# Regrouping the output products of a cross-attention kernel: A12·B21 in the queries' PSUM bank, S2·T2 on top of P1, and the fourth batch's x one slot sooner

## The chip, the cores and the metric

The kernel runs on one core of a Trainium2 chip. The number of interest is the device time of one execution in microseconds. The core has five engines that run their own instruction queues in order: TensorE (PE, with its weight loads shown as PEld), VectorE (DVE), ScalarE (ACT), GpSimd (POOL) and SyncE (SP), which here only issues DMAs. They wait for each other by semaphores. All data is float32.

## The reference

For eight batches of 256 rows and 1024 features the kernel computes layer norm, a query projection, attention of 32 heads over a context that serves as keys and as values, an output projection and the residual sum:

```python
x = (hidden_states - mu) * jax.lax.rsqrt(var + LN_EPS) * ln_gamma + ln_beta
Q = _split_heads(x @ Wq.T)
K = _split_heads(memory_keys)
V = _split_heads(memory_values)
scores = jnp.einsum('bhsd,bhtd->bhst', Q, K) * scale
scores = jnp.where(mask, scores, -jnp.inf)
probs = jax.nn.softmax(scores, axis=-1)
attn = jnp.einsum('bhst,bhtd->bhsd', probs, V)
out = attn.transpose(0, 2, 1, 3).reshape(B, S, HIDDEN) @ Wout.T
return residual + out
```

## The kernel before

**Slots.** The work is cut into 64 slots, eight for each batch; a slot handles one group of four heads (128 features). The loop `for n in range(N)` writes the instructions of slot n, and since every engine takes its instructions in order, the order of this text is the order of the work. The scheduler is off (`manual_schedule`), so nothing is reordered. In slot n PE first computes the scores of group n+1 (`scores`, L479), then the values of group n-2 (`values`, L622), and around them parts of other products; meanwhile DVE, ACT and POOL do the softmax of group n+1 (`softmax_parts`).

**Softmax.** `exps` is a DVE pass with the mask (L515) and an ACT exponential (L519) for each half of four heads; `normalize` is a DVE reciprocal (L526) and two POOL multiplications (L528); `blocks` transposes with DVE (L534) into pT, and `aside` copies a part with ACT into pc (L540). The `tail` then lets SP swap partition quarters by DMA: two pT<-pT (L600), then two pT<-pc (L604). Between the two pairs SP issues the loads listed in `between`, which fills the wait for the first pair. `values` of a group can start only when its pT is complete. `copy_at` moves a group's values from PSUM to SBUF (ACT, L635).

**Queries.** For batches 0 to 2 `make_q` (L340) multiplies plain blocks of x with Wq; ACT copies the result out with `copy_q` (L347 to L353). From batch 3 on the query projection is a seven-product form of the 2x2 block product (`query_product`, L440): one product a slot in seven of eight slots, emptied by `copy_product` (L450, L456, L461). All go through one PSUM bank, pool `ps_q`; the second halves made during batch 0 and 1 use the output bank, pool `ps_o`. The x of a batch is loaded some eleven slots ahead (`load_x`, L130), its statistics are DVE work (`ln_stats`, L226), its rearrangement is DMA work (`move_x`, L327).

**Output projection.** For each batch, in the eight slots after its own attention began to finish, `product_steps` (L694) runs seven products of four matmuls each: P1 = A11·B11, A12·B21, S2·T2, S3·T3, A22·T4, S1·T1, S4·B22. Here A are quarters of the attention output, B quarters of Wout, and S and T are sums of them (`sum_at` on POOL L675, `sum_wo` on POOL L183). The four quarters of the result are: C11 = P1 + A12·B21; the other three are P1 + S2·T2 plus further products. `STEPS` gives for each slot i of the batch how many steps stand before the values, after them, and at the slot's end. In every batch but the last two, A12·B21 is added in the bank that holds P1. `keep_p1` (ACT, L702) copies P1 to SBUF first; S2·T2 then starts a new bank, and POOL adds the kept P1 to three quarters of the residual (`add_p1`, L727). `store`, `take` (DVE, L732 to L736) add a bank to the residual tile r, and `store` also sends it.

**Order around the change.** In slot i=1 of a batch the order on PE is scores, four A11, values, three A12; in slot i=2 scores, values, the last A12, the query product, two S2. `copies` stands for the emptying of query banks: early in the softmax in the first eight groups, at its end later. The loads of Wout (`load_wo`), of x, of k, v and of the residual (`load_res`) are put into `between` of chosen slots, in this order.

Of the kernel before, what the change touches and what calls it, by code (L numbers as in the profile page):

```python
# [59 lines left out]
def xattn_kernel(  # L60
# [11 lines left out]
    nc = tc.nc  # L72
# [4 lines left out]
    NQ = NC  # L77
# [160 lines left out]
        else:  # L238
            later.append(pow_)

    def ln_norm(b, s, engine):
        if engine is nc.scalar:
            shift = sm.tile([P, 1], F32, tag="shift", name=f"shift_{b}_{s}", bufs=2)
            nc.gpsimd.tensor_scalar(
                shift, mvs[b][:, s, 0:1], rstds[b][:, s : s + 1], -1.0, ALU.mult, ALU.mult
            )
            engine.activation(
                xs[b][:, s, :], xs[b][:, s, :], AF.Identity,
                bias=shift, scale=rstds[b][:, s : s + 1],
            )  # L250
            return
        engine.tensor_scalar(
            xs[b][:, s, :], xs[b][:, s, :], mvs[b][:, s, 0:1], rstds[b][:, s : s + 1],
            ALU.subtract, ALU.mult,
        )

# [234 lines left out]
    def softmax_parts(n, copies=(), ahead=(), between=(), hooks={}, fill=()):  # L491
# [50 lines left out]
        if n == 0:  # L542
            for j in range(NH - 1):
                exps(j, (0,))
            yield
            exps(NH - 1, (0,))
            fill_in()
            yield
            for j in range(NH):
                exps(j, (1,))  # L550
            normalize(0)
            fill_in()
        else:
            exps(0)
            while tails:
                tails.pop()()
            late = "p1" in hooks
            if not late:
                for done in list(pvs):
                    copy_at(done)  # L560
            exps(1)
            for hook in hooks.get("soon", ()):
                hook()
            exps(2)
            normalize(0)
            for hook in hooks.get("p1", ()):
                hook()
            exps(3)
            if late:
                for done in list(pvs):  # L570
                    copy_at(done)
        if n <= NQ:
            for copy in copies:
                copy()
        for hook in hooks.get(0, ()):
            hook()
        normalize(1)
# [10 lines left out]
        blocks(2)  # L588
        while fill:
            fill_in()  # L590
        if n > NQ:
            for copy in copies:
                copy()

        def tail():
            blocks(3)
# [48 lines left out]


    PRODUCTS = (
        ("A11", B11, True), ("A12", B21, False), ("S2", T2, True), ("S3", T3, False),
        ("A22", T4, False), ("S1", T1, True), ("S4", B22, False),
    )  # L650

    STEPS = ((0, 0, 0), (4, 0, 3), (0, 1, 2), (0, 2, 2), (0, 2, 1), (0, 1, 2), (0, 0, 3), (0, 1, 2),
             (0, 2, 0))
    ENDS = ((0, 0, 2), (0, 0, 5), (0, 0, 5)) + ((0, 0, 4),) * 4 + ((0, 0, 0),)
    ENDS_TO = {2: (0, 0), 3: (0, 1), 4: (1, 1), 5: (1, 0), 6: (1, 1), 7: (0, 1)}
# [18 lines left out]
            operand(b, name)[:, c], operand(b, one)[:, c], operand(b, two)[:, c], op  # L676
        )

    s2s, p1s = {}, {}

    def product_steps(b, steps):
        for step in steps:
            p, c = divmod(step, NK)
            name, which, begins = PRODUCTS[p]
            po = pos.get(b)
            if b == B - 2 and name in ("A12", "S2"):

                begins = name == "A12"
                if begins and c == 0:
                    po_q[0] = ps_q.tile([P, 512], F32, tag="pq", name=f"po_{b}_{name}")  # L690
                po = po_q[0] if begins else po
            elif begins and c == 0:
                po = pos[b] = ps_o.tile([P, 512], F32, tag="po", name=f"po_{b}_{name}")
            nc.tensor.matmul(  # L694
                po, operand(b, name)[:, c], wo[:, which, c],
                start=begins and c == 0, stop=c == NK - 1,
                skip_group_check=not begins,
            )
# [3 lines left out]
        nc.scalar.copy(p1s[b], pos[b])  # L702


    po_q, ends_kept = [None], {}

    def copy_po(b, i):
        if "tile" not in ends_kept:
# [3 lines left out]
        nc.scalar.copy(ends_kept[i], pos[b])  # L712

    def take_po_q(b):
        nc.vector.tensor_tensor(p1s[b], po_q[0], p1s[b], ALU.add)
        ends_kept[2] = p1s[b]

    def add_kept(b, i, s, h):
# [10 lines left out]
    def take(b, s, h):  # L729

        r = rs[b, s, h]
        nc.vector.tensor_tensor(r, pos[b], r, ALU.add)  # L732

    def store(b, s, h, po=None):
        r = rs.pop((b, s, h))
# [54 lines left out]
    for b in range(1, B):  # L790
        first = NQ * (b - 1) + 2
        if b == 1:
            when = dict(moves=())
        elif b == 2:
            when = dict(
                loads=(0, 1), stats=(2, 3), norms=(3, 3), trans=(4, 5),
                moves=tuple(5 + (i + 2) // 6 for i in range(16)),
            )
        else:
            when = dict(  # L800
                loads=(first - 12, first - 11) if b == SPLIT else (first - 13, first - 12),
                stats=(first - 10, first - 9) if b == SPLIT else (first - 11, first - 9),
                norms=(first - 8, first - 7), trans=(first - 7, first - 6),
                moves=tuple(first - 6 + (i + 2) // 6 for i in range(16)),
            )
# [12 lines left out]
        if b % 2 == 0:  # L818
            masks[NQ * b - 7].append(b)
# [30 lines left out]

    ln_stats(0, 0)
    ln_stats(0, 1, (0,))
    ln_norm(0, 0, nc.vector)
    ln_stats(0, 1, (1, 2))
    transpose_x0(0)
    early, late = (0, 1, 5, 2, 6, 3), (7, 4)
    for c in early + late:
        copy_x0(0, c, nc.vector if c > 4 else nc.scalar)
    nc.gpsimd.tensor_copy(xnT0[:, :, S], bet)
    ln_norm(0, 1, nc.vector)  # L860
    first_q(0, early + late)
    mask_bias(0)
    transpose_x0(1)
# [20 lines left out]
    for b in range(B - 1):  # L884
        done, ends = 0, b == B - 2
        for i, counts in enumerate(ENDS if ends else STEPS):
            n = NQ * (b + 1) + i
            for place, k in enumerate(counts):
                steps.setdefault((n, place), []).append((b, range(done, done + k)))
                done += k  # L890
        for i, *what in (
            ((2, keep_p1), (3, take_po_q), *((i, copy_po, i) for i in range(3, 8))) if ends else
            ((1, keep_p1), (2, store, 0, 0), (3, take, 0, 1), (4, take, 1, 1), (6, store, 1, 0),
             (7, store, 1, 1), (8, store, 0, 1))
        ):
            evacuations[NQ * (b + 1) + i].append((what[0], b, *what[1:]))
# [6 lines left out]
    for n in range(N):  # L903
# [8 lines left out]
        if n + 3 in firsts or n + 2 in firsts:  # L912
            between, ahead = between + ahead, []
        if b >= 0:
            if b == B - 2 and i - 1 in (5, 6):
                between.append(partial(send, b, *ENDS_TO[i - 1]))
            if i < 4 and b + i > 0:
                between.append(partial(load_res, b, *((0, 0), (0, 1), (1, 1), (1, 0))[i]))
        between += [partial(load_x, *args) for args in loads[n]]
        between += [partial(load_mask, one) for one in masks[n]]  # L920
        for which, pair in {
            0: ((B12, 0),), 1: ((B22, 0),), 2: ((B11, 0), (B12, 1)), 3: ((B22, 1),),
            4: ((B11, 1), (B21, 0)), 5: ((B21, 1),),
        }.get(n, ()):
            between.append(partial(load_wo, which, pair))
        if n == NQ - 2:
            between.append(partial(load_res, 0, 0, 0))
        if n == N - 4:
            again = xp.tile([P, NS, D], F32, tag="x", name="x_again")
# [22 lines left out]
        if n in products:  # L952
            query_product(*products[n])
            copies.append(partial(copy_product, *products[n]))
        for one in now:
            one()
        fill = []
        if n < 2:
            transpose_x1(2 * n)
# [5 lines left out]
        if n + 1 < N:  # L965
            softmax(n + 1, copies, ahead, between, hooks, fill)
        else:
            copy_at(n - 2)
            for load in between:
                load()  # L970
        if b >= 0 and i == 1:
# [30 lines left out]
        if b == B - 2:  # L1002
            if i > 2:
                add_kept(b, i, *ENDS_TO[i])
        elif b >= 0 and i in (3, 4, 5):
            add_p1(b, *{3: (0, 1), 4: (1, 1), 5: (1, 0)}[i])
        for one in later:
            one()
        if n in halves and n % 2:
# [32 lines left out]
    )  # L1042
    end_steps(to_c11, "A12", B21, (0,), (0,))
    end_steps(to_c21, "A22", T4, (0,), (0,))
    end_steps(to_c22, "S1", T1, (0,), (0,))
    end_steps(to_c11, "A12", B21, (1,))
    end_steps(to_c21, "A22", T4, (1,))
    values(N - 2)
# [8 lines left out]
    copy_at(N - 1)  # L1057
    end_sum(slice(3, 4), nc.vector)
    first_cols, last_cols = slice(0, 384), slice(384, 512)
    end_steps(to_c22, "S1", T1, (1,))  # L1060
    end_steps(s2t2, "S2", T2, (2,))
    for r in (r01, r10, r11):
        end_add(r, s2t2)
# [61 lines left out]
```

## Time and profile before

| | |
|---|---|
| median of 3 runs | 577.23 us (575.44 to 579.26) |
| the profiled execution's own time | 577.06 us |
| its span in the profile | 575.3 us, mean granted clock 0.997 |
| PE busy | 567.5 us, 99% of the span |
| DVE busy | 459.1 us, 80% |
| ACT busy | 411.6 us, 72% |
| POOL busy | 403.8 us, 70% |
| DMA | 117.98 MB, mean 205 GB/s |

Busy time is a sum over the span; matmuls are pipelined, so a busy PE is not PE at its peak. The span is the profiled execution from its first to its last instruction; its own time is 1.8 us longer. A line such as "PE po_A L694 <- ACT qa L349: 2.7, 1, 2.7" in the view of waits says who waited for whom, how long in all, how often, and the longest. In the chain of work each line gives start, length and the instruction that had to end before the next could go on. In the timeline a line gives start, length, engine, source line, operation, tiles, shapes and, in brackets, the idle time of the engine before it and what ended it. A 128x512 matmul is recorded as two records, a group of values as 64.

### The profile page before, as it was taken

The numbers are of one execution on the slowest core, as the hardware profiler recorded it, in microseconds if no ns is written. First come the engines' busy times: TensorE is split into PE (matmuls) and PEld (weight loads), VectorE is DVE, ScalarE is ACT, GpSimd is POOL, SyncE is SP. The second block draws the span as 40 slices with busy tenths as digits, with TensorE's granted clock in tenths as the row PEclk, the third lists the DMA queues.
The fourth block names the chain that finished last, engine by engine and source line by source line (L and its number), as shares of the span: only waits on it lengthen the run. The fifth ranks groups of instructions, "written<-read, shape, count | busy, mean of one in ns | idle before, by whom it ended". The sixth has DMA issues, their size and how long they took to land.

```text
span 575.3 us, 20001 instructions
## 1 busy us (share of the span) xinstructions
PE 567.5 (99%) x7162; PEld 393.2 (68%) x7162; DVE 459.1 (80%) x1696; ACT 411.6 (72%) x1424; POOL 403.8 (70%) x675
## 2 busy tenths in 40 slices
PE   8999998999999999999999999999999999999997
PEld 8778884667667777677676677667766767755444
DVE  5897986888877879889888888888877868879824
ACT  3697886677667867698667967778766876769820
POOL 1788896899896896766567675666657657448780
PEclk9999998999999999999999999999999999999999
DMA  8667877666778677877677776897568865536751
GB/s 303 233 191 234 236 223 200 203 194 187 191 235 270 202 199 194 252 227 222 182 230 230 214 204 195 241 272 203 144 182 267 241 196 138 140 107 180 205 163 74
DMA packets 47475, 117.98 MB, mean 205 GB/s; under 512 B 9104, under 2 KB 9872, under 8 KB 47376
## 3 DMA queue, kind: packets, MB, share of 16 engines
q1 hardware_dynamic: 47088, 116.69, 68.8%
q8 instruction: 57, 0.93, 0.7%
q14 instruction: 42, 0.34, 0.2%
q10 hardware_dynamic: 288, 0.01, 0.0%
HBM read 65.28 MB, written 11.53 MB: 134 GB/s over the span
## 4 chain that ended last, share of the span: by engine, by line
PE 84%; DMA 4%; POOL 4%; DVE 3%; ACT 2%; issue 1%; SPq 1%; DVEq 0%; ACTq 0%
PE po_S L694 20%; PE pq_A L440 16%; PE po_A L694 11%; PE pv L622 11%; PE sc L479 10%; PE pq L340 7%; PE pq_S L440 6%; PE po_end L761 2%; POOL e L528 2%; DMA wq<-in_wq_dram 2%; DMA x<-in_x_dram 1%; DVE e L515 1%; ACT e L519 1%; DVE pT L534 1%; PE po_last L761 1%
## 5 line engine op out<-in xcount | busy, mean ns | idle before, releaser
L528 POOL TENSOR_SCALAR e<-e,rden 128x256 f32<-128x256 f32 x512 | 235.7, 478 | 129.5 <-DVE rden L526 127.5
L519 ACT ACTIVATE e<-e,mn 128x256 f32<-128x256 f32 x512 | 254.0, 500 | 49.4 <-DVE mn L515 48.3
L534 DVE STREAM_TRANSPOSE pT<-e 128x512 f32<-128x512 f32 x256 | 180.7, 707 | 54.0 <-POOL e L528 34.8
L515 DVE CUSTOM_DVE_ANT_0 e<-sc,mb 128x256 f32<-128x256 f32 x512 | 186.0, 416 | 24.2 <-PE sc L479 23.6
L540 ACT COPY pc<-pT 128x512 f32<-128x512 f32 x128 | 79.0, 617 | 72.1 <-DVE pT L534 42.4
L519 ACT ACTIVATION_READ_ACCUMULATOR e<-e,mn 128x1 f32 x512 | 97.8, 191 | 0.0
L340 PE MATMUL pq<-xnT,wq 128*128 128x256 f32 (+1 forms) x368 | 84.1, 382 | 0.0
L340 PEld LDWEIGHTS pq<-xnT,wq 128*128 128x128 f32 x368 | 68.7, 190 | 14.3 <-issue 4.0
L479 PEld LDWEIGHTS sc<-k,qa 32*128 32x128 f32 x1024 | 46.1, 184 | 42.4 <-issue 22.0
L622 PE MATMUL pv<-pT,v 64*32 64x128 f32 x4096 | 74.5, 274 | 0.2
L622 PEld LDWEIGHTS pv<-pT,v 64*32 64x32 f32 x4096 | 57.0, 105 | 25.6 <-issue 11.6
L694 PE MATMUL po_S<-wo,at 128*128 128x512 f32 x152 | 74.3, 606 | 0.0
L479 PE MATMUL sc<-k,qa 32*128 32x256 f32 x1024 | 73.6, 400 | 0.1
L694 PE MATMUL po_A<-wo,at 128*128 128x512 f32 x128 | 62.4, 622 | 2.7 <-ACT qa L349 2.7
L694 PE MATMUL po_S<-wo,s 128*128 128x512 f32 x104 | 50.1, 605 | 0.0
L526 DVE RECIPROCAL rden<-den 128x2 f32<-128x2 f32 x256 | 37.7, 147 | 6.6 <-ACT e L519 5.3
L515 DVE DVE_READ_ACCUMULATOR2_ANT mn<- 128x1 f32 x512 | 42.7, 83 | 0.0
L694 PEld LDWEIGHTS po_A<-wo,at 128*128 128x128 f32 x128 | 23.2, 195 | 28.3 <-issue 23.2
L440 PEld LDWEIGHTS pq_A<-xnT,wq 128*128 128x128 f32 x320 | 37.3, 192 | 4.8 <-issue 4.1
L694 PEld LDWEIGHTS po_S<-wo,at 128*128 128x128 f32 x152 | 25.8, 190 | 19.8 <-issue 19.3
L440 PE MATMUL pq_A<-xnT,wq 128*128 128x128 f32 x320 | 37.3, 275 | 0.0
L635 ACT COPY at<-pv 128x128 f32<-128x128 f32 x128 | 26.1, 253 | 9.6 <-PE pv L622 9.6
(95 smaller groups left out, 605.9 us busy)
## 6 DMA issues: line engine op xcount, KB each, us to landing
v<-in_kv_dram SPq DMA_DIRECT2D x32, 512.0 KB, 4.6
pT<-pT SPq DMA_DIRECT2D x128, 128.0 KB, 2.9
pT<-pc SPq DMA_DIRECT2D x128, 128.0 KB, 4.1
ring<-kept_T SPq DMA_DIRECT2D x18, 512.0 KB, 5.3
k<-in_kv_dram SPq DMA_DIRECT2D x32, 256.0 KB, 4.2
x<-in_x_dram SPq DMA_DIRECT2D x14, 512.0 KB, 5.6
r<-in_x_dram SPq DMA_DIRECT2D x28, 256.0 KB, 4.7
out_dram<-r SPq DMA_DIRECT2D x28, 256.0 KB, 3.4
```

What stands on the lines that cost most here:

```text
L340: nc.tensor.matmul(pqs[n], wq[:, o, c, :], xnTs[b](c), start=(c == 0), stop=(c == NC - 1),)
L440: nc.tensor.matmul(pqs[b][:, o, :], w[:, c], x_[:, c], start=begins and o + c == 0, stop=c == NK - 1, skip_group_check=True,)
L479: nc.tensor.matmul(scs[n][j][:, s, :], qa[r, n % NQ, ts(s, P)], ks[n - n % 2][r, n % 2, :], start=True, stop=True,)
L515: nc.vector.tensor_tensor_reduce(out=e[:, s, :], in0=pss[j][:, s, :], in1=mbs[n // NQ], scale=1.0, scalar=NO_SCORE, op0=ALU.add, op1=ALU.m ...
L519: nc.scalar.activation(e[:, s, :], e[:, s, :], AF.Exp, bias=mn[:, s : s + 1], scale=-1.0, accum_out=den[:, s : s + 1],)
L526: nc.vector.reciprocal(rden, dens[j])
L528: nc.gpsimd.tensor_scalar(es[j][:, s, :], es[j][:, s, :], rden[:, s : s + 1], 1.0, ALU.mult, ALU.mult,)
L534: nc.vector.transpose(pT[:, :, :, j, :, :].rearrange("p a i s k -> p (a i) s k"), es[j].rearrange("p s (b t) -> p b s t", t=K),)
L540: nc.scalar.copy(pc[:, :, ts(j, 2)], pT[:, 1, :, ts(j, 2)])
L622: nc.tensor.matmul(pvs[n][r][j * HD : (j + 1) * HD], vs[n - n % 2][ts(r, 2 * K), i, ds(n % 2 * P + j * HD, HD)], pT[ts(r, 2 * K), :, i, j, ...
L635: nc.scalar.copy(ats[b, k][:, c, :, ts(r, 2), :], pv.rearrange("p a s k -> p s a k"))
L694: nc.tensor.matmul(po, operand(b, name)[:, c], wo[:, which, c], start=begins and c == 0, stop=c == NK - 1, skip_group_check=not begins,)
```

## The change

Seven things are different:

- A12·B21 gets its own bank in every batch: the queries' bank, `ps_q`. S2·T2 is added on top of P1 in the output bank. P1 therefore is added by POOL only to quarter (0, 0), in slot i=2, and DVE's new `take_q` adds the A12·B21 bank to the same quarter.
- That quarter is sent from the `between` list of slot i=3 instead of at once.
- `STEPS`: slot i=1 runs all of A11 and three of A12 after the values, slot i=2 the last A12 and two S2 before the query product. In batch 1 the query product of slot 17 stands between A11 and A12.
- In the softmax the copy of values goes back ahead of the second exponential in all slots, the copy of P1 goes behind the last one, and the query copies of slots with that copy, and the first one of slot 8, go ahead of the rest.
- Batch 3's x is loaded in slots 5 and 6 instead of 6 and 7; four pieces of Wout and the first residual tile are loaded one slot later.
- At the start x of batch 0 is normalised in halves.
- At the end the last slot's copy of a result goes behind the copy of values, and the first S1·T1 step of the last batch goes behind the last values.

```diff
@@ softmax_parts @@
-            late = "p1" in hooks
-            if not late:
-                for done in list(pvs):
-                    copy_at(done)
+            for done in list(pvs):
+                copy_at(done)
             exps(1)
             for hook in hooks.get("soon", ()):
                 hook()
             exps(2)
             normalize(0)
-            for hook in hooks.get("p1", ()):
-                hook()
             exps(3)
-            if late:
-                for done in list(pvs):
-                    copy_at(done)
-        if n <= NQ:
-            for copy in copies:
-                copy()
+        for hook in hooks.get("p1", ()):
+            hook()
+        copies = list(copies)
+        for copy in copies[: NQ if n <= NQ or "p1" in hooks else 1 if n == NQ + 1 else 0]:
+            copies.remove(copy)
+            copy()
...
-        if n > NQ:
-            for copy in copies:
-                copy()
+        for copy in copies:
+            copy()
@@ products and steps @@
-        ("A11", B11, True), ("A12", B21, False), ("S2", T2, True), ("S3", T3, False),
+        ("A11", B11, True), ("A12", B21, True), ("S2", T2, False), ("S3", T3, False),
...
-    STEPS = ((0, 0, 0), (4, 0, 3), (0, 1, 2), (0, 2, 2), (0, 2, 1), (0, 1, 2), (0, 0, 3), (0, 1, 2),
+    STEPS = ((0, 0, 0), (0, 7, 0), (0, 3, 0), (0, 2, 2), (0, 2, 1), (0, 1, 2), (0, 0, 3), (0, 1, 2),
@@ product_steps @@
-            if b == B - 2 and name in ("A12", "S2"):
-
-                begins = name == "A12"
-                if begins and c == 0:
-                    po_q[0] = ps_q.tile([P, 512], F32, tag="pq", name=f"po_{b}_{name}")
-                po = po_q[0] if begins else po
+            if name == "A12":
+
+                if c == 0:
+                    po_q[b] = ps_q.tile([P, 512], F32, tag="pq", name=f"po_{b}_{name}")
+                po = po_q[b]
...
+    def take_q(b, s, h):
+        r = rs[b, s, h]
+        nc.vector.tensor_tensor(r, po_q[b], r, ALU.add)
@@ loads @@
-                loads=(first - 12, first - 11) if b == SPLIT else (first - 13, first - 12),
+                loads=(first - 13, first - 12),
...
-            0: ((B12, 0),), 1: ((B22, 0),), 2: ((B11, 0), (B12, 1)), 3: ((B22, 1),),
-            4: ((B11, 1), (B21, 0)), 5: ((B21, 1),),
+            0: ((B12, 0),), 1: ((B22, 0),), 2: ((B11, 0),), 3: ((B12, 1),),
+            4: ((B22, 1), (B11, 1)), 5: ((B21, 0),), 6: ((B21, 1),),
         }.get(n, ()):
             between.append(partial(load_wo, which, pair))
-        if n == NQ - 2:
+        if n == NQ - 1:
             between.append(partial(load_res, 0, 0, 0))
@@ start @@
-    ln_norm(0, 0, nc.vector)
+    for h in range(2):
+        ln_norm(0, 0, nc.vector, ts(h, 512))
...
@@ evacuations and the loop @@
+            if (b, i) == (1, 1):
+                counts = (0, 4, 3)
...
-            ((1, keep_p1), (2, store, 0, 0), (3, take, 0, 1), (4, take, 1, 1), (6, store, 1, 0),
+            ((1, keep_p1), (2, take_q, 0, 0), (3, take, 0, 1), (4, take, 1, 1), (6, store, 1, 0),
...
+            if b < B - 2 and i == 3:
+                between.append(partial(send, b, 0, 0))
...
-        for one in now:
-            one()
+        if n + 1 < N:
+            for one in now:
+                one()
...
             copy_at(n - 2)
+            for one in now:
+                one()
...
-        elif b >= 0 and i in (3, 4, 5):
-            add_p1(b, *{3: (0, 1), 4: (1, 1), 5: (1, 0)}[i])
+        elif b >= 0 and i == 2:
+            add_p1(b, 0, 0)
@@ end @@
-    end_steps(to_c22, "S1", T1, (0,), (0,))
...
-    end_steps(to_c22, "S1", T1, (1,))
+    end_steps(to_c22, "S1", T1, range(2), (0,))
```

More of the change, by code (lines that the diff above doesn't have):

```diff
@@ L239, in ln_stats, with ln_norm @@
             later.append(pow_)
-    def ln_norm(b, s, engine):
+    def ln_norm(b, s, engine, cols=slice(0, D)):
         if engine is nc.scalar:
@@ L252, in ln_norm @@
         engine.tensor_scalar(
-            xs[b][:, s, :], xs[b][:, s, :], mvs[b][:, s, 0:1], rstds[b][:, s : s + 1],
+            xs[b][:, s, cols], xs[b][:, s, cols], mvs[b][:, s, 0:1], rstds[b][:, s : s + 1],
             ALU.subtract, ALU.mult,
@@ L677, in sum_at @@
         )
-    s2s, p1s = {}, {}
+    s2s, p1s, po_q = {}, {}, {}
     def product_steps(b, steps):
@@ L702, in keep_p1 @@
         nc.scalar.copy(p1s[b], pos[b])
-    po_q, ends_kept = [None], {}
+    ends_kept = {}
     def copy_po(b, i):
@@ L714, in take_po_q @@
     def take_po_q(b):
-        nc.vector.tensor_tensor(p1s[b], po_q[0], p1s[b], ALU.add)
+        nc.vector.tensor_tensor(p1s[b], po_q[b], p1s[b], ALU.add)
         ends_kept[2] = p1s[b]
@@ L859, in xattn_kernel @@
     nc.gpsimd.tensor_copy(xnT0[:, :, S], bet)
-    ln_norm(0, 1, nc.vector)
+    for h in range(2):
+        ln_norm(0, 1, nc.vector, ts(h, 512))
     first_q(0, early + late)
```

## The prediction

> **What bounds the kernel now.** I read the engine totals, then the waits of TensorE, then the chain of work where the one long wait lies. The totals:
>
> ```profile
> span 575.3 us, 20001 instructions
> PE 567.5 (99%) x7162; PEld 393.2 (68%) x7162; DVE 459.1 (80%) x1696; ACT 411.6 (72%) x1424; POOL 403.8 (70%) x675
> ```
>
> Busy PE alone proves nothing, so who PE waited for in the whole run:
>
> ```profile
> PE po_A L694 <- ACT qa L349: 2.7, 1, 2.7
> PE busy L120 <- POOL ring masks.py:199: 1.3, 1, 1.3
> PE po_end L761 <- POOL ring L753: 0.4, 1, 0.4
> ```
>
> Three waits, 4.4 us together. Everywhere else PE has its next matmul ready: the inner batches repeat every 68.1 us (po_A starts at 233.30 and 301.42 us in the chain), with no idle PE. So a change to another engine is worth nothing until it moves one of these waits, and a new wait on PE is paid in full. The long one, in the chain of work:
>
> ```profile
> 90.48 0.59 DVE st L226
> 91.07 0.61 DVE pT L534
> 91.68 0.01 DVE rden L526
> 91.69 0.02 issue
> 91.72 0.62 ACT pc L540
> 92.33 0.39 ACT qa L349
> 92.72 0.04 issue
> 92.76 5.26 PE po_A L694 x8
> ```
>
> The first A11 product of slot 9 needs a bank that ACT empties at 92.7, behind DVE, which stood 2.7 us for x:
>
> ```profile
> DVE st L226 <- DMA x<-in_x_dram: 2.7, 1, 2.7
> ```
>
> The stretches around it (busy us of each engine, granted clock, DMA share, GB/s) show a second price:
>
> ```profile
> 88.80:92.70 3.90, 1.23 (x17) 0.72 (x16) 3.47 (x9) 0.98 (x3) 1.81 (x4) 0.98 1.02 288
> 92.70:96.20 3.50, 3.44 (x5) 1.57 (x6) 3.41 (x17) 3.04 (x12) 3.50 (x5) 0.54 0.52 136
> ```
>
> The clock is 0.54 after the gap. The eight records take 5.26 us, the same eight 3.63 in later batches: 1.63 more. This place costs 2.73 + 1.63 = 4.36 us.
>
> **The change part by part.** Matmuls stay the same in number; their places change. Prices on PE, from the chain at 230 to 260 us: scores 1.08, values 1.09, one 128x512 matmul 0.86, a query product 3.57, and 0.19 whenever full matmuls follow scores or values (po_A 3.63 for four after scores, 3.44 without).
>
> *One run of output steps.* Slot i=1 was scores, A11, values, A12; it becomes scores, values, A11, A12, with one change to full matmuls instead of two: -0.19 in each of six batches. For the four inner batches, 2 to 5, that is -0.76; batches 0 and 1 are summed below.
>
> *Slot 9 (batch 0).* Three edits remove the old wait: x is loaded a slot sooner, so DVE need not stand; ACT copies the first query bank before its other work; A11 stands behind the values. What is late next? The values of head group 7, now first, and the transfers that complete pT_7. The queue of SP:
>
> ```profile
> 81.63 1.16 SPq L600 DMA_DIRECT2D pT<-pT  x2
> 82.84 0.58 SPq L136 DMA_DIRECT2D k<-in_kv_dram  x1
> 83.46 0.45 SPq L130 DMA_DIRECT2D x<-in_x_dram  x1
> 83.95 0.43 SPq L150 DMA_DIRECT2D r<-in_x_dram  x1
> 84.48 1.15 SPq L604 DMA_DIRECT2D pT<-pc  x2
> ```
>
> The two pT<-pc at the end complete pT_7. By the trace's semaphore counts fifteen of the second one's sixteen parts have landed at 90.3 and the last at 92.4. Today nobody cares: the values start at 97.95. After the change PE is ready for them at 90.0. And the moved loads stand in this queue: in this group x stays (its other half), the residual (256 KB) goes a slot later and a 512 KB piece of Wout takes its place. That is 256 KB more ahead of pT<-pc; at the 288 GB/s of the row above, 0.9 us. So the copies land at 93.3, or at 91.2 if no part is a straggler.
>
> From there PE has 1.09 + (0.19 + 4x0.86) + 3x0.86 = 7.3 us of slot 9, where before slot 10 began at 101.81. With 93.3 slot 10 begins at 100.6 if the clock stays full and at 102.3 if it is halved for the same 3.4 us, in which 1.7 are lost. [...] I go by the row: 102.3, a loss of 0.5. Bounds: 97.3 (copies in time) is a gain of 4.5; a landing 1 us later still with the gate is a loss of 1.5.
>
> *Slot 8.* The same shift puts 512 KB of x ahead of the pT<-pc issued at 75.71, which landed by 80.8. At the same 288 GB/s that is 1.8 us: 82.6, against values that start at 82.41. I take 0.0, since part of the queue then drained (transfers ran above 350 GB/s near 76); bounds 0 to 1.0.
>
> *Other moved DMAs.* Four of the eight Wout pieces go one slot later. The last, of B21, now leaves SP near 84 and would land near 91 (6.5 us, the median of such loads); its first reader, A12's third matmul, comes near 98 at the soonest. The residual of batch 0 lands in slot 8 and is first read in slot 10. The output of r00 is no longer sent in slot i=2 but in the group of slot i=3, behind pT<-pT and v and ahead of the next residual: 0.53 us of SP issue, taken from one slot and put in the next. Cover: SP stands up to 4.4 us for pT<-pT in such groups. Each at 0.
>
> *Slot 17 (batch 1)* holds a query product in the same queries' bank that A12 now wants. PE: 160.59 + 1.08 + 1.09 + 3.63 + 3.45 = 169.84. ACT's copy took 170.14 to 170.62, 0.2 after the product ended; now A12 waits for it: 169.84 + 0.2 + 0.48 + 0.07 = 170.6, a wait of 0.75. Queued behind it are A12 and all the next scores. Less the 0.19: +0.5. Bounds 0.3 to 1.0.
>
> *The new wait in slot i=2.* The query product there needs the bank that A12 leaves only when DVE has added it to r00 (take_q). Before, the old store read another bank and nothing queued behind it. In batch 2: slot 25 starts at 232.16 and lasts 8.38, so slot 26 starts at 240.54, A12 ends at 243.76, S2's two matmuls at 245.48, and then pq_S may wait. DVE in slots 25 and 26 now:
>
> ```profile
> 238.16 0.71 DVE L534 STREAM_TRANSPOSE pT<-e 128x512 f32<-128x512 f32 x1 [1.65 <-PE pv L622]
> ...
> 243.11 0.41 DVE L515 CUSTOM_DVE_ANT_0 e<-sc,mb 128x256 f32<-128x256 f32 x1
> ...
> 244.48 0.69 DVE L736 TENSOR_TENSOR r<-po_A,r 128x512 f32<-128x512 f32 x1
> ```
>
> The 1.65 us wait for pv goes, as values come first. Then ACT's exps (234.19 + 8x0.495 + 0.4 for the copy of values put ahead = 238.55) and POOL set the last transpose at 240.4; statistics take 1.6 (to 242.0), four score passes 1.4 (to 243.4), then A12's end at 243.8, then 0.7: take_q ends at 244.5, 1.0 us before PE asks. With today's DVE times it would end at 245.17, still 0.3 early. So 0; bounds 0 to 0.7 a batch.
>
> *Covered work.* S2 is read 3.6 us sooner: POOL finished it at 242.09, PE asks at 243.76. Keep_p1 now follows all exps, until 239.2 against 243.76. POOL loses two of three adds of P1 a batch (2x1.28 us), all beside PE: 0. The one it keeps, behind S4, falls in 2.41 us of idle time. Without the cover it would be 1.28 a batch.
>
> *Start and end.* x is normalised in halves; the transposes begin at 7.72, when PE's 32 warming matmuls end (7.9), while the whole normalisation ended at 6.92: 0, at most -0.25. At the end a product that waited for POOL is put behind the last values: -0.43, bounds -0.5 to 0.
>
> *Sum:* +0.5 - 0.76 + 0.5 - 0.43 = -0.2. The profiled run took 577.06 (span 575.3 and 1.8 around it), so 576.9; the median of the runs is 577.23, 0.17 above it: **577.0**. Within 1% (5.8 us) is about what a measurement of this kernel can tell from no change.
>
> **The rivals.** *The transfers are in time (0.20).* If pT_7 has landed by 90.0, slot 9 gains 4.5: 577.23 - 4.5 - 0.76 + 0.5 - 0.43 = 572.0, and 571.4 with the halves at the start and less wait in slot 17. For it: fifteen of sixteen parts were there at 90.3, and the copies were issued while x still moved. Against it: the DMA share of 1.02, and more bytes ahead.
>
> *take_q is late (0.34), the slower case.* Place: the query product of slot i=2, six batches. It decides once take_q ends after PE's request, 1.0 us later than worked out, and then every us is paid six times, with all PE work queued behind. If DVE or r00's landing is 2.5 us late (DVE stood 2.9 us once for a transfer), each batch loses 1.5: 577.0 + 9 = 586. At 1.0 us each the 1% is reached. For it: DVE is the second busiest engine, at 80%, and slack on PE is the only slack removed in every batch. Against it: the pv wait of 1.65 goes.
>
> *The edit only trades one wait for another (0.46)* is my forecast, 572 to 582 by its bounds. That the steps don't move as described is excluded: each engine's order of instructions shows them moved.
>
> **Numbers.** Forecast 0.46, in time 0.20, late 0.34. Faster by over 1%: two thirds of the second case and a little of the first, 0.15. Slower: nearly all of the third, 0.33. The rest 0.52. Range 571.5 to 586: it leaves out the tail of the second case and the upper third of the late one, under 2 in 10.
>
> **What would show it.** PE's waits: po_A <- ACT qa gone; pv <- a transfer in slot 9, at 92 to 94 us; po_A <- ACT qa of 0.7 near 170; po_end's wait gone. [...] pq_S or pq_A waiting for DVE r in slot i=2 every 68 us would mean the slower rival. Inner batches of 67.9 us mean the steps, of 69.5 and more the rival. I am wrong if PE finds pT_7 ready, or if a bank wait repeats.

## The result, and the profile after

The changed kernel takes 578.16 us (median of 20 runs, 575.33 to 582.16), the kernel before, in the runs beside it, 576.36 us (20 runs, 573.76 to 579.26). The ratio is 1.0038, with a 95% interval of 1.002 to 1.0057: slower, by about 2 us. The prediction was 577.0, a change of -0.2; the time lies inside its range and within the 1% that it held likeliest, but the sign is wrong, and the difference is beyond its interval.

The profiled execution of the changed kernel (576.73 us) is 1.4 us quicker than the median of its runs. Its totals and its waits of PE (us in all, times, longest):

```profile
span 574.9 us, 19980 instructions
PE 566.6 (99%) x7162; PEld 393.9 (69%) x7162; DVE 462.1 (80%) x1698; ACT 411.5 (72%) x1424; POOL 389.4 (68%) x663
```

```profile
PE pv L617 <- DMA pT<-pT: 2.9, 1, 2.9
PE busy L120 <- POOL ring masks.py:199: 1.3, 1, 1.3
PE po_A L688 <- ACT qa L353: 0.6, 1, 0.6
PE px L266 <- DVE x L252: 0.3, 1, 0.3
```

The wait of po_A for qa of 2.7 us is gone, and so is the short one of po_end; in their place the values of slot 9 wait 2.9 us for pT. The other two new waits are the one of slot 17 and one from halving the normalisation at the start. Slot 9 in the timeline of PE (start, length, what, and in brackets the idle time before it):

```profile
88.77 1.15 PE L479 MATMUL sc<-k,qa 32*128 32x256 f32 x16
92.83 1.67 PE L617 MATMUL pv<-pT,v 64*32 64x128 f32 x64 [2.91 <-DMA pT<-pT]
94.43 7.79 PE L688 MATMUL po_A<-wo,at 128*128 128x512 f32 x14
102.15 1.15 PE L479 MATMUL sc<-k,qa 32*128 32x256 f32 x16
```

and the granted clock around it, whose fall to about half (0.54 in the stretch of before) the forecasts call the gate (stretch, its length, busy us of PE, PEld, DVE, ACT and POOL, granted clock, DMA share, GB/s):

```profile
88.77:92.80 4.03, 1.15 (x17) 0.72 (x17) 3.85 (x18) 2.58 (x7) 3.95 (x6) 1.00 1.03 249
92.80:96.50 3.70, 3.64 (x67) 2.07 (x68) 0.96 (x6) 2.00 (x9) 2.39 (x4) 0.68 0.56 163
96.50:98.50 2.00, 2.00 (x5) 0.85 (x4) 1.82 (x5) 1.38 (x6) 1.90 (x5) 0.75 0.56 131
```

The seven output steps (14 records) take 7.79 us here and 6.28 in later batches. The queue of SP behind that wait, with the DMA engines full (DMA share 1.03), and the time from issue to landing of the two pT<-pc at 84.97:

```profile
82.06 1.21 SPq L595 DMA_DIRECT2D pT<-pT  x2
83.48 0.42 SPq L136 DMA_DIRECT2D k<-in_kv_dram  x1
83.95 0.44 SPq L130 DMA_DIRECT2D x<-in_x_dram  x1
84.44 0.43 SPq L173 DMA_DIRECT2D wo<-in_woT_dram  x1
84.97 1.15 SPq L599 DMA_DIRECT2D pT<-pc  x2
```

```profile
DMA to landing us min/median/max: 7.6/7.7/7.7
```

These two copies complete pT_7. By the trace's semaphore counts their last parts landed at 92.69 and 93.15, and the first matmul of the values starts at 92.83. The name in the brackets, pT<-pT, is a wrong one: one of the two pT<-pT of the next group, issued at 86.79, counts on the same semaphore as a copy of pT_7 that had landed at 84.74, and was in the middle of landing. In all seven traces in which the values of slot 9 waited, they began 0.09 to 0.14 us after the first pT<-pc of their own group had landed, whatever name the brackets give.

So in this execution the site went as forecast: slot 10 began at 102.15, forecast 102.3, before 101.81. Against this one pair of traces the whole sum is right too. It is the pair that misleads, as more traces show.

### The profile page after: what moved, and what is told of

The parts are those of the page before. It is cut to its first block, busy times and chain, and to the rows that moved or that the text cites. A ratio compares the mean times of both kernels' runs of the same rounds, so it can differ in the third digit from the quotient of the medians.

```text
span 574.9 us, 19980 instructions
## 1 busy us (share of the span) xinstructions
PE 566.6 (99%) x7162; PEld 393.9 (69%) x7162; DVE 462.1 (80%) x1698; ACT 411.5 (72%) x1424; POOL 389.4 (68%) x663
## 4 chain that ended last, share of the span: by engine, by line
PE 86%; DMA 5%; POOL 4%; DVE 2%; ACT 2%; issue 1%; SPq 0%; DVEq 0%; ACTq 0%
PE po_A L688 22%; PE pq_A L440 16%; PE pv L617 11%; PE sc L479 10%; PE po_S L688 9%; PE pq L340 7%; PE pq_S L440 6%; PE po_end L759 3%; POOL e L528 2%; DMA x<-in_x_dram 1%; DMA wq<-in_wq_dram 1%; ACT e L519 1%; PE po_last L759 1%; DVE e L515 1%; DMA pT<-pT 1%
## 5 line engine op out<-in xcount | busy, mean ns | idle before, releaser
L688 PE MATMUL po_A<-wo,at 128*128 128x512 f32 x224 | 108.5, 613 | 0.6 <-ACT qa L353 0.6
L688 PEld LDWEIGHTS po_A<-wo,at 128*128 128x128 f32 x224 | 39.6, 193 | 38.3 <-issue 35.9
L688 PE MATMUL po_S<-wo,s 128*128 128x512 f32 x56 | 26.9, 606 | 0.0
L688 PE MATMUL po_S<-wo,at 128*128 128x512 f32 x56 | 26.9, 605 | 0.0
L688 PE MATMUL po_A<-wo,s 128*128 128x512 f32 x56 | 26.8, 603 | 0.0
```

Source lines behind the costliest of these rows:

```text
L688: nc.tensor.matmul(po, operand(b, name)[:, c], wo[:, which, c], start=begins and c == 0, stop=c == NK - 1, skip_group_check=not begins,)
```

## The experiments

A slot is measured from the start of its scores on PE to the start of the next ones. All traces repeat each other within 0.1 us in slots 1 to 6 and from slot 11 to the last, but for slot 17, the slots i=1 (where the change takes off 0.19 us) and the slots i=2 spoken of below. The slots between, in us; without any wait they would take 7.54, 7.54, 8.57 (8.37 with A11 behind the values) and 8.39. "Full clock" counts the runs whose mean granted clock was 0.999 or more. The kernel before had a full clock in 61 of 115 such runs, counted over its second trace's runs and those beside the experiments (two of over 581 us are left out), and among the 35 of the first group its median was 575.48 with a full clock and 578.35 with one loss (mean 0.997).

| kernel | x a slot sooner | A11 behind values | 7 | 8 | 9 | 10 | runs at full clock | ratio to before |
|---|---|---|---|---|---|---|---|---|
| before, first trace | no | no | 7.54 | 7.54 | 12.93 | 8.39 | | |
| before, again | no | no | 8.17 | 7.54 | 9.77 | 8.42 | 7 of 12 | 1.0003 (0.9973 to 1.0032) |
| changed, first trace | yes | yes | 7.54 | 7.66 | 13.38 | 8.39 | 3 of 20 | 1.0038 (1.002 to 1.0057) |
| changed, again | yes | yes | 9.01 | 14.04 | 8.54 | 8.39 | 3 of 12 | 1.0014 (0.9986 to 1.0042) |
| residual early | yes | yes | 7.54 | 8.29 | 14.19 | 8.39 | 1 of 12 | 1.0031 (1.0006 to 1.0057) |
| A11 first | yes | no | 7.54 | 8.73 | 8.99 | 9.97 | 8 of 12 | 0.9997 (0.9966 to 1.0029) |
| all loads of before | no | yes | 8.39 | 7.54 | 11.97 | 8.39 | 8 of 12 | 0.9967 (0.9941 to 0.9994) |
| before with the new loads | yes | no | 7.88 | 8.60 | 8.57 | 10.41 | 9 of 12 | 0.9976 (0.9953 to 0.9999) |
| old loads and A11 first | no | no | 8.53 | 7.94 | 8.56 | 11.90 | 11 of 12 | 0.9982 (0.9953 to 1.001) |
| before, early copy | no | no | 7.62 | 7.59 | 11.46 | 8.39 | 9 of 12 | 0.9981 (0.9955 to 1.0007) |
| PE filled | yes | yes | 7.54 | 8.82 | 12.25 | 8.39 | 10 of 12 | 1.003 (1.0005 to 1.0056) |
| Wout as before | yes | yes | 7.54 | 8.59 | 9.44 | 8.39 | 7 of 12 | 0.9993 (0.9963 to 1.0022) |
| x as before | no | yes | 7.54 | 7.54 | 10.60 | 8.39 | 2 of 12 | 1.0024 (0.9998 to 1.0051) |
| put together | no | yes | 7.54 | 7.54 | 13.85 | 8.42 | 7 of 12 | 0.9969 (0.9939 to 0.9999) |

The experiments were run in groups of four on one chip each, with runs of the kernel before beside them (medians 576.29, 577.51 and 575.95); compare by the ratio, not by the time.

**Both kernels again, unchanged.** 

> The kernel before once more, unchanged, for a second trace and for the spread of its clock. Theory 1 (slot 9 decides): the wait of po_A for ACT qa near 90 and the gate after it vary from run to run, and the profiled run shown so far, 577.06 against a median of 576.4, was on the dear side; this trace has a wait between 0 and 2.8 us there. Theory 2 (the residual decides): slot 9 is as before, 2.6 to 2.8 us of wait and a halved clock. Time within 0.3% of the kernel before under both.

> The changed kernel once more, unchanged. Its first trace agreed with the sum of the prediction (slot 10 began 0.34 us later than before, the span was 0.4 us shorter), but its median is 1.8 us over that of before. Theory 1: pT_7 lands later in a typical run than the 92.8 us of the first trace, so that PE stands over 3 us in slot 9 at a halved clock; the rest of the trace repeats within 0.2 us. Theory 2: slot 9 repeats within 0.3 us, and a query product of some slot i=2 (near 178, 246, 314, 382, 450) waits 0.5 to 2 us for DVE r, which waits for the residual; the first trace had 0.5 to 0.8 us of slack there.

The kernel before took 575.99 us. In its second trace the same bank kept PE waiting 0.97 us instead of 2.73, and the clock stayed full:

```profile
92.00 3.70 PE L694 MATMUL po_A<-wo,at 128*128 128x512 f32 x8 [0.97 <-ACT qa L349]
```

```profile
92.00:95.60 3.60, 3.60 (x8) 1.43 (x8) 3.57 (x19) 3.13 (x11) 3.60 (x4) 1.00 0.79 266
```

The cost of the old site is thus 4.36 us in one execution and 1.2 in another (9.77 against 8.57). The changed kernel took 577.76, 1.0014 of the runs beside it, which alone would not tell it from no change (0.9986 to 1.0042). Its second trace lost its time one slot sooner, at the values of slot 8:

```profile
86.02 0.38 PE L617 MATMUL pv<-pT,v 64*32 64x128 f32 x2 [2.22 <-ACT e L519]
87.72 1.95 PE L617 MATMUL pv<-pT,v 64*32 64x128 f32 x62 [1.32 <-issue]
89.60 7.16 PE L340 MATMUL pq<-xnT,wq 128*128 128x256 f32 x24
```

The brackets mislead here too: by the semaphore counts the last parts of the two pT<-pc of pT_6 landed at 85.92 and 87.63, so both waits were for them. The 24 query matmuls take 7.16 us instead of 5.45: the clock is halved again (0.57, 0.50, 0.50 and 0.72 in stretches of 2 us from 86.0 on). By these numbers it was at 0.50 for 6.8 us, twice as long as after the gaps in the first traces (92.55 to 95.92 before, 94.11 to 97.51 changed, 3.4 us each). From the start of slot 10 to the end it is 472.75 and 472.77 us in the two traces of the changed kernel, 473.49 and 473.64 in those of before. The part of the change that lies there gains 0.7 to 0.9 us; slots 7 to 9 hold most of the difference between these four executions. Theory 1 expected slot 9 to be the place; it was slots 8 and 9. Theory 2, the residual, showed nothing in this trace.

**A11 ahead of the values in slot 9, all else changed.**

```diff
+            if (b, i) == (0, 1):
+                counts = (4, 0, 3)
```

> In batch 0 alone the four A11 steps stand before the values in slot 9, as in the kernel before; all else as in the changed kernel. ACT has emptied the bank at 89.6, so A11 fills the time in which PE stood. Both theories: the wait for pT and the halved clock go, slot 10 begins at 97.5 to 98.5 instead of 102.15. Theory 1: the time falls by 4 to 6 us below the changed kernel, to 572 to 574, about 0.993 of the kernel before. Theory 2: by 4 only, and the excess of some 2 us over the sum stays: 574 to 575.

576.61 us, and the clock full in 8 of 12 runs instead of 6 of 32. The wait of slot 9 went:

```profile
90.48 3.70 PE L688 MATMUL po_A<-wo,at 128*128 128x512 f32 x8
94.16 1.54 PE L617 MATMUL pv<-pT,v 64*32 64x128 f32 x64
...
104.72 2.64 PE L340 MATMUL pq<-xnT,wq 128*128 128x256 f32 x11 [1.10 <-DVE r L730]
```

The expected 4 to 6 us were not there. 1.19 us stayed in slot 8, and 1.58 came back in slot 10, where PE now arrived before DVE had taken the queries' bank: the wait of the slower rival, at the first batch.

**The residual a slot sooner.** r00 of batches 1 to 5 is loaded in slot i=7 of the batch ahead.

> The residual r00 of batches 1 to 5 is loaded one slot sooner; all else as in the changed kernel. Theory 2: DVE's take of the queries' bank no longer waits for the load, the time falls by 1.5 to 2 us to 576 to 576.5. Theory 1: no change beyond 0.1%, about 578; if anything slower, since the 256 KB now stand ahead of pT in slot i=7, where nothing waited.

578.32 us, 1.0031 of before: no gain, as theory 1 had it, with 3.82 us of wait for pT in slot 9. The residual was not what slowed the typical run.

**The loads of before in the changed kernel.**

```diff
-                loads=(first - 13, first - 12),
+                loads=(first - 12, first - 11) if b == SPLIT else (first - 13, first - 12),
...
-            0: ((B12, 0),), 1: ((B22, 0),), 2: ((B11, 0),), 3: ((B12, 1),),
-            4: ((B22, 1), (B11, 1)), 5: ((B21, 0),), 6: ((B21, 1),),
+            0: ((B12, 0),), 1: ((B22, 0),), 2: ((B11, 0), (B12, 1)), 3: ((B22, 1),),
+            4: ((B11, 1), (B21, 0)), 5: ((B21, 1),),
...
-        if n == NQ - 1:
+        if n == NQ - 2:
```

> The changed kernel with the loads of before: batch 3's x in slots 6 and 7, Wout and the first residual tile where they were. The two traces of the changed kernel have 28.6 and 31.6 us from slot 7 to slot 10, those of before 28.0 and 25.5, and what follows slot 10 is 0.8 shorter in the changed kernel in all of them. Theory L (the earlier loads delay pT_6 and pT_7): slots 7 to 10 take 24 to 26.5 us, two runs in three or more keep the full clock, the median falls to 574 to 576. Theory S (A11 behind the values uncovers pT_7 whatever is loaded): slot 9 still has a wait of 1.5 to 3 us for pT and a halved clock in most runs, 576.5 to 578.

575.55 us, 0.9967 of before, the clock full in 8 of 12. Without the earlier loads the regrouping is a gain. Slot 8 has no wait in this trace; slot 9 still waits for pT_7, and the clock was lost on that (11.97 us). So theory S names the place and theory L has the median and the clock, though slots 7 to 9 of this trace, 27.9 us, lie above its 24 to 26.5:

```profile
91.99 0.38 PE L617 MATMUL pv<-pT,v 64*32 64x128 f32 x2 [1.19 <-DMA pT<-pc]
92.75 1.91 PE L617 MATMUL pv<-pT,v 64*32 64x128 f32 x62 [0.38 <-issue]
```

**The new loads alone, in the kernel before.** The same lines, the other way.

> The kernel before with the loads of the changed kernel alone: batch 3's x in slots 5 and 6, four pieces of Wout and the first residual tile a slot later. Theory L: the values of slot 8 wait 0.5 to 3.5 us for pT, more runs lose clock than the 13 of 35 of before, and the median rises to 577 to 579. Theory S: slot 8 waits at most 0.5, the wait of po_A for ACT qa falls below 1 us since DVE has its x, and the median falls to 574.5 to 576.

576.85 us, 0.9976 of before. Each theory had a half of this: slot 8 waits as theory L says (8.60 us), but the old wait of slot 9 goes altogether, as theory S says, and 9 of 12 runs keep the clock. What is won is again partly given back in slot 10, to a transfer of x:

```profile
83.43 0.38 PE L622 MATMUL pv<-pT,v 64*32 64x128 f32 x2 [0.43 <-issue]
84.01 1.13 PE L622 MATMUL pv<-pT,v 64*32 64x128 f32 x62 [0.21 <-issue]
...
104.09 3.69 PE L340 MATMUL pq<-xnT,wq 128*128 128x256 f32 x16 [1.78 <-DMA xnT<-xe]
```

So neither the loads nor the order of A11 alone makes the kernel slower; the two together do. The traces show why. With A11 behind them, the values come first in slot 9 and need the two pT<-pc at once, and the loads push these back: from issue to its last part the second one took 6.8 to 8.1 us in the seven traces with the later piece of Wout in this group (median 7.6), 4.9 to 7.6 in the other seven (median 5.9). The ranges overlap, so the loads make a late landing more frequent; they are not its only cause.

**Old loads and A11 first.** Both edits above in the changed kernel.

> The changed kernel with the loads of before and, in batch 0, with A11 ahead of the values in slot 9. A11's bank is emptied before DVE stands for x, and pT_7 has 3.6 us more. Both theories: no wait over 0.5 us in slots 8 and 9, 23.7 to 24.5 us from slot 7 to slot 10, clock full in nearly all runs. By the sum 73.6 + 24 + 473 + 1.8 = 572.4: median 572 to 574. If the wait that slot 10 showed in the run with A11 first (1.1 us for DVE r) stays, 574.

575.57 us, 0.9982: full clock in 11 of 12, but not 572. The traced execution is the slowest of the twelve (579.11), so what it paid is more than the typical run paid. Slot 10 paid 3.5 us, first for S2 on POOL and then for DVE, which had stood 4.6 us for x in slot 8:

```profile
103.61 1.98 PE L688 MATMUL po_A<-wo,s 128*128 128x512 f32 x4 [1.87 <-POOL s L670]
106.69 3.50 PE L340 MATMUL pq<-xnT,wq 128*128 128x256 f32 x15 [1.10 <-DVE r L730]
```

The same trace shows the slower rival inside the batches. In slots 26 and 34 DVE waits for the residual, and the query product behind A12's bank waits for DVE. DVE and PE in slot 26:

```profile
246.42 0.69 DVE L730 TENSOR_TENSOR r<-po_A,r 128x512 f32<-128x512 f32 x1 [2.17 <-DMA r<-in_x_dram]
```

```profile
247.16 3.84 PE L440 MATMUL pq_S<-sx,ring 128*128 128x128 f32 x32 [0.85 <-DVE r L730]
```

Slots 26 and 34 take 9.62 and 9.89 us instead of 8.50. This happened in two of the eight traces that have the new bank and load the residual as the changed kernel does (the other is "Wout as before", with 0.48 and 0.83 us), and in neither of the two with the earlier residual. A third trace, "x as before", lost 0.2 us in slot 34, where DVE had stood 1.24 us for the residual. Slot 26 is not free of waits with the old bank either: it took 8.69, 9.08 and 8.95 us in three of the four traces that have it, 0.2 to 0.6 over its length, where PE stood at A12's last matmul. What the new bank adds is thus less than the 2.6 us of this one trace.

**The early copy of the query bank alone, in the kernel before.**

```diff
-        if n <= NQ:
-            for copy in copies:
-                copy()
+        copies = list(copies)
+        for copy in copies[: NQ if n <= NQ else 1 if n == NQ + 1 else 0]:
+            copies.remove(copy)
+            copy()
...
-        if n > NQ:
-            for copy in copies:
-                copy()
+        for copy in copies:
+            copy()
```

> The kernel before with one edit: in the softmax of slot 8 the first copy of a query bank goes ahead of the rest on ACT, as in the changed kernel. Both theories: the wait of po_A for ACT qa near 90 goes, slots 7 to 10 take 23.7 to 25, the clock is full in nearly all runs: 573 to 574.5. If that wait was not what cost the clock, 576.

575.91 us, 0.9981. A11 did start at once (90.29), but slots 7 to 9 took 26.7 us, not 23.7 to 25: the same lateness returned behind the values: DVE still stood 2.7 us for x, and A12 waited for ACT's copy of P1.

```profile
97.91 2.84 PE L694 MATMUL po_A<-wo,at 128*128 128x512 f32 x6 [2.83 <-ACT p L702]
```

```profile
95.00:97.90 2.90, 0.08 (x5) 0.00 (x0) 1.65 (x12) 2.90 (x12) 2.90 (x4) 1.00 0.42 105
97.90:99.00 1.10, 1.09 (x3) 0.61 (x4) 0.76 (x2) 1.10 (x6) 1.10 (x3) 1.00 0.37 91
```

This gap of 2.83 us cost no clock.

**PE filled.** Three more 128x512 matmuls ahead of the values of slot 9, into a bank that A12 then overwrites.

```diff
+        if n == NQ + 1:
+            po_q[0] = ps_q.tile([P, 512], F32, tag="pq", name="po_0_A12")
+            for c in range(3):
+                nc.tensor.matmul(
+                    po_q[0], operand(0, "A11")[:, c], wo[:, B11, c], start=True, stop=True,
...
-                if c == 0:
+                if c == 0 and b:
```

> The changed kernel with three more 128x512 matmuls (A11 operands, into the queries' bank, thrown away by A12's first matmul) ahead of the values in slot 9: 2.6 us of work in the time in which PE stood for pT_7. If the halved clock is the price of the idle gap, PE does not idle there, the clock stays full in more runs than the 6 of 32 of the changed kernel, and three matmuls more make the kernel faster: 576 to 577. If the time is lost in the wait alone and the clock has another cause, no change or 1 us slower: 578 to 579, 6 of 32 as before. A wait in slot 8 stays under both.

```profile
91.45 2.84 PE L950 MATMUL po_A<-wo,at 128*128 128x512 f32 x6
95.07 1.43 PE L617 MATMUL pv<-pT,v 64*32 64x128 f32 x64 [0.77 <-DMA pT<-pc]
96.42 6.28 PE L688 MATMUL po_A<-wo,at 128*128 128x512 f32 x14
```

The clock was full in 10 of 12 runs, against 6 of 32 of the changed kernel, and the 14 records take 6.28 us again (clock 1.00 from 93 to 99 us): idle PE is what costs the clock here. But the time was 577.28 us, between the two forecasts and 1.003 of before, no better than the changed kernel by the ratios. The filler is 2.6 us of work in every run, also where pT_7 comes early; that this outweighs the clock won is argued, not measured run by run.

**The loads split.** Only Wout and the first residual as before, x sooner; then only x as before.

> The changed kernel with Wout's pieces and the first residual tile where they were in the kernel before; x stays a slot sooner. Undoing all loads gave 575.55, or 0.9967 of before. If the bytes ahead of pT_7 in its own group decide (a 512 KB piece of Wout in place of a 256 KB residual), this alone brings 575 to 576 and 8 of 12 runs at full clock. If x a slot sooner decides, 577 to 578 and under half at full clock.

> The changed kernel with batch 3's x in slots 6 and 7 as before; Wout and the residual stay a slot later. The other half of the split: if x a slot sooner decides, 575 to 576 with 8 of 12 runs at full clock; if the piece of Wout in pT_7's group decides, 577 to 578. If both halves cost about the same, each of these two runs lies between, near 577.

576.65 us (0.9993) with 7 of 12 at full clock, and 577.16 (1.0024) with 2 of 12. The waits of the values in slots 8 and 9 of the first, and in slot 9 of the second:

```profile
83.37 1.62 PE L617 MATMUL pv<-pT,v 64*32 64x128 f32 x64 [0.52 <-DMA xnT<-xe]
...
91.95 0.38 PE L617 MATMUL pv<-pT,v 64*32 64x128 f32 x2 [0.51 <-ACT pc L540]
```

```profile
92.15 1.58 PE L617 MATMUL pv<-pT,v 64*32 64x128 f32 x64 [1.74 <-DMA pT<-pT]
```

Here too the values waited for their own pT<-pc, not for what the brackets name. The clock leans to Wout's 512 KB in pT_7's own group as the dearer half, and so do the second pT<-pc, 4.9 us from issue to landing with Wout as before and 6.8 with x as before; the two times do not tell the halves apart, since their intervals overlap. Slot 8 does tell about x: in the seven traces with x a slot sooner it takes 7.66 to 14.04 us, median 8.60; in the seven with x in its old place 7.54, with 7.59 and 7.94 the only exceptions. Slot 7 waited in six traces, four of them with x in its old place, which no run here explains; over both slots the medians still differ by 1.1 us.

**Put together.** The changed kernel with all loads of before, the residual r00 early, and in slot 17 the query product ahead of A11, with ACT's copy ahead of that of P1:

```diff
-                counts = (0, 4, 3)
+                counts = (0, 0, 0, 7)
...
+        project_steps(n, 3)
```

> The changed kernel with all loads of before, the residual r00 of batches 1 to 5 a slot sooner, and in slot 17 the query product ahead of A11 with ACT's copy ahead of P1's. Against the run with the old loads (575.55, slot 17 12.66 us, 26 to 34 67.93): slot 17 falls to 11.9 to 12.0 us, no query product in slots 26, 34 and 42 waits for DVE r, slots 7 to 10 as there. By the sum 575.55 - 0.65 = 574.9; 574 to 576, below both kernels.

574.88 us, 0.9969 of before (0.9939 to 0.9999), below both kernels, though by the ratio no lower than with the old loads alone (0.9967); what slot 17 gained is seen in the trace only. Slot 17 fell from 12.66 to 11.82 us, more than the 0.65 expected, because the steps now also stand in one run, and no inner batch waits:

```profile
163.46 3.72 PE L340 MATMUL pq<-xnT,wq 128*128 128x256 f32 x16
167.02 6.17 PE L688 MATMUL po_A<-wo,at 128*128 128x512 f32 x14
```

Slot 9 is not cured. In its trace, with the loads of before, the values waited 3.33 us for pT, longer than in the first trace of the changed kernel, and the clock was lost after that; 7 of 12 runs kept it.

## Why the prediction was wrong

**The sign.** The step that failed is the price of the old place: "This place costs 2.73 + 1.63 = 4.36 us". That is what one execution paid. In the second trace of the kernel before the site cost 1.2, and 61 of its 115 runs lost no clock at all. The forecast weighed a new wait with a lost clock against an old one with a lost clock and found +0.5. What it had to weigh was a kernel that loses the clock in 26 of 32 runs against one that does so in about half. With slot 8, set to nothing (below), this is what turned a small gain into a loss.

**Slot 8.** "I take 0.0": the bound was 0 to 1.0, and it measured 0.12 us in the first trace of the changed kernel and about 1.1 as the median of the seven traces with the earlier x. The working gave 82.6 against 82.41 and was then set to nothing because the queue drained for a while; a landing at the edge of its need is worth the spread of that landing, not the difference of two single times. The upper bound was too low: the second trace paid 6.5, 3.5 of it idle and the rest at the halved clock (0.50 and 0.57).

**The size.** Of a hundred runs 34 more lose the clock (81 against 47), at the 2.9 us that separate runs with and without it in the first group of before (3.5 and 3.6 in the other two): 1.0 to 1.2 us. With 1.1 in slot 8 that makes 2.1 to 2.3 beside the forecast -0.2, or about +2; the first runs say +2.2 by the ratio and +1.8 by the medians, the second runs +0.8 by the ratio. The two terms overlap where slot 8 itself loses the clock, so this is an estimate. That the loads and the order of slot 9 together are the cause is shown from both sides: the old loads, or A11 first, each bring the clock back in 8 of 12 runs, and the ratio to 0.9967 and 0.9997. How the loss divides between slots 8 and 9 in the runs without a trace is not known.

**Slot 9, mechanism.** Right in place, cause and size for the first trace: the pT<-pc of pT_7 were forecast for 93.3 and landed at 92.69 and 93.15; the clock fell to 0.68 and then 0.75 in the two stretches; slot 9 grew by 0.45, forecast 0.5. That the second trace did not wait here at all, since slot 8 had already cost it 6.5, the forecast did not have. The rival that the transfers are in time fails in the first trace; for runs without a trace the clock does not decide it, since a wait of 1.74 us for pT_7 ("x as before") kept the full clock.

**The clock.** That a gap of this length costs the clock the forecast took from the row of before: 2.73 us, and 0.54 after it. For the site that was right: 2.91 us lost the clock too (down to 0.50), and so did 3.33 (0.50, "put together") and 3.82 (0.59 and 0.55, "residual early"). The 3.4 us at half the clock came again as well, from 94.11 to 97.51. But among the gaps under 3 us the length alone does not decide: 2.83 ("before, early copy") and 1.74 ("x as before") kept 1.00, while 1.19 and 0.38 with a few values between lost it (0.72 and 0.50, "all loads of before"), as did 2.22 and 1.32 (0.57 and 0.50, "changed, again"). What else decides, no run here shows.

**The steps in one run.** Forecast -0.19 a batch; slots 25, 33, 41 and 49 fell from 8.57 to 8.37 and the inner period from 68.12 to 67.92. Right.

**Slot 17.** Forecast +0.5, from a wait of 0.75 and a saving of 0.19; measured +0.65. The view gives 0.57 of idle time:

```profile
166.56 3.62 PE L340 MATMUL pq<-xnT,wq 128*128 128x256 f32 x16
170.75 2.84 PE L688 MATMUL po_A<-wo,at 128*128 128x512 f32 x6 [0.57 <-ACT qa L353]
```

From start to start, though, the query product takes 4.19 us here and 3.46 where nothing waits behind it: the wait costs 0.73, nearly the forecast. The saving came as well (A11 and the query product are each 0.10 shorter from start to start than in the kernel before), but A12 is 0.11 longer behind the wait. That last term the sum did not have. In the last kernel nothing waits in slot 17, and it is 0.19 shorter than before (11.82 against 12.01).

**take_q.** Forecast: no wait, 1.0 us of slack. In both traces of the changed kernel PE did not wait, but in slot 26 of the first the slack was 0.5, because DVE had stood 0.70 us for the residual:

```profile
245.09 0.69 DVE L730 TENSOR_TENSOR r<-po_A,r 128x512 f32<-128x512 f32 x1 [0.70 <-DMA r<-in_x_dram]
```

The rival was right in its mechanism and wrong in its frequency: it asked for a wait in six batches, and where it came inside them (in two traces of variants), it came in two of the inner batches, at 0.5 to 1.1 us of wait.

**Start and end.** In the first pair of traces slot 0 begins 0.23 us sooner (22.21 instead of 22.44), just inside the bound of -0.25; but over all traces it begins at 21.75 to 22.83 with the change and at 22.44 to 22.79 without, so a gain is not shown. From the scores of the last slot the end gained 0.65 us (35.03 against 35.68), of which the forecast had the 0.43 of the wait; the rest, 0.22, would fit one change to full matmuls fewer (0.19); no run separates it.

## What to carry to other kernels

The stretch at 88 to 92 us, with a DMA share of 1.01 to 1.03 and several engines waiting for transfers, had no single price (4.36 us in one execution of the kernel before, 1.2 in another): take two or three traces of such a place, and the granted clock of every run, before a wait there is entered into a sum. When a wait is removed by moving a load forward, look at what the load is moved past, and when a product is moved behind another, at what that other one waits for; each may be harmless and the two together not (here 0.9976 of before with the loads alone, 0.9967 without them, 1.0038 together). And a gain at such a place can be taken back by the next stage: three variants without the wait of slot 9 paid 1.6 to 3.5 us in slot 10, and a fourth paid it behind the values.

## What the runs showed of the hardware

The same kernel on the same chip spread over 5 to 7 us, though nearly all of its slots repeat within 0.1 us; about 1 us of the spread lies ahead of slot 0 (in the traces it begins between 21.75 and 22.83), the rest in a few slots near 75 to 105 us, where the DMA share reached 1.03 (88 to 92 us). A pair of 128 KB copies there took 7.7 us from issue to landing (from 84.97), against a median of 4.0 over the run for copies of that line. A lost clock could be counted without a trace: a mean granted clock of 0.997 is 1.7 us of 575, one such loss as the traces show it, and 0.994 is two: the one trace with 0.994 has the half clock for 6.8 us. And more work could keep the clock: three matmuls whose result is thrown away brought it back in 10 of 12 runs, without winning time.
